# Pricing image parts with TensorE durations from the trace, and Silu and Softplus in halves, in a planned four-layer kernel

## The chip, the cores and the metric

The kernel runs on one core of a Trainium2 chip. The metric is the device time of one execution in microseconds (us). The core has TensorE (PE; its weight loads are shown as PEld), VectorE (DVE), ScalarE (ACT), GpSimd (POOL) and SyncE (SP), each with its own instruction stream that is worked off in order, and DMA queues. Semaphores tie the streams together.

## The reference

The input is a batch of 8 images of 56 x 56 pixels and 192 channels, in float32. Four layers follow each other, each as `x = x + layer(group_norm(x))`:

1. A gated layer with long convolutions: `p = silu(x @ p_w)`, `qv = silu(x @ q_w) * silu(x @ v_w)`, two Toeplitz products of `qv` along the rows and along the columns of the image, `(p * (o1 + o2)) @ o_w`.
2. Attention with 6 heads in shifted windows of 7 x 7 pixels.
3. A depthwise convolution of 3 x 3.
4. A selective scan: a projection to two times 384 channels (`x` and `z`), a depthwise convolution and Silu on `x`, then for each of 4 directions `delta = softplus(dt + bias)`, the recurrence `h = exp(delta * A) * h + (delta * x) * B` along the 3136 tokens for each of 16 states, `y = sum(h * C) + D * x`; the directions are added, normalized, multiplied with `silu(z)` and projected back.

## The kernel before, in words

**Set-up.** The Toeplitz coefficients are made, then `products` and `toeplitz` do the first layer's convolutions for four images; for the other four they run beside the front of the first image.

**The front of an image** is all that has to be done before its scan can start. It is a Python generator, `front(b)`, made of five: `gate` (the rest of layer 1: per chunk of 448 tokens 12 matmuls for `p`, an Identity activation for each of 6 blocks at line 490, one Silu over all six at 492, 48 transposing matmuls at 503, a product on VectorE at 511, 12 matmuls at 516), `attention` (lines 596 to 691), `conv2` (depthwise matmuls at 780), `inner` (input projection at 840, depthwise convolution at 869, two Silu over 3136 tokens at 886, a transposing copy at 892) and `steps` (14 passes: a projection at 918, six small matmuls at 928, six Identity activations at 933, one Softplus over 2688 columns at 937, two stores). After each Silu and Softplus `usual_functions()` (line 342) loads the table that has Exp and Ln again. Each `yield held, needs, wait` ends a part: how many PSUM banks it holds, how many the next part needs, and how long its loads take.

**The scan loop** goes over 8 images x 4 directions ("slots") x 7 chunks = 224 chunks, and in each over 3 blocks of 128 channels and 8 groups of two states: 24 pairs a chunk, 672 an image. For one pair: POOL multiplies `du` with `bm` into one of the 6 slots of `ring` (line 1059), ScalarE sets the initial state (1066, for three pairs at once), forms `exp(delta * A)` in PSUM (1076, two banks' worth of buffers) and keeps the last state (1098); VectorE scans (1085); POOL (for every other pair) or VectorE multiplies the states with `cm` into `hc` (1091, 4 buffers); PE adds them up over the states with an identity matrix (1106, two matmuls that show as four instructions). When a chunk's block is done, `sums` adds it to `ysum` (1116 to 1118). When an image's last direction is under way, `finish` (lines 950 to 1001) normalizes and writes out.

**The planner.** The loop is written out under a manual schedule: what Python emits first stands first in an engine's stream. While it emits pairs, `Parts` keeps a clock for each of the engines P, A, D and E (POOL, ScalarE, VectorE, TensorE) in `self.t`, and `run(engine, cost, *after)` moves one on. The pairs' own costs are written out: 1.78 for POOL, 1.3 for ScalarE's exponentials, 2.02 for a scan, 1.1 for the sum on PE. The costs of the image parts are not: the first image's front runs before the loop, and while it does, every instruction goes through `Meter` and `MeteredEngine`, which note (engine, price) for each part. Those logs are the prices for the fronts of the seven other images. Once a pair, `step` asks `fits` for each open front or finish whether its next part may be emitted now. It may if, with its price added, ScalarE's clock stays 0.7 us before the end of the next scan and TensorE's within 5.0 us after its start; a part that has been refused gets 3 us of grace for each refusal. The next front starts when the one before it has ended. If an image's first `steps` pass is not made when the loop needs it, the front is run on without limits until it is.

The change touches `TIMES`, `call` in `MeteredEngine`, the Silu of `gate` and `inner`, the Softplus of `steps`, the cost in `sums`, and the cost of `add_up` (the `run("E", 1.1, ...)` near the end of the loop).

Of the kernel before, what the change touches and what calls it, by code (L numbers as in the profile page):

```python
# [23 lines left out]
L = H * W  # L24
# [20 lines left out]
class Meter:  # L45


    TIMES = {"tensor": ("E", 0.04, 1.25e-3), "scalar": ("A", 0.2, 0.83e-3),
             "vector": ("D", 0.1, 1.05e-3), "gpsimd": ("P", 0.1, 2.25e-3)}

    def __init__(self, nc):
# [9 lines left out]
class MeteredEngine:  # L61
# [3 lines left out]
    def __getattr__(self, name):  # L65
        f = getattr(self.it, name)
        engine, base, each = self.times

        def call(*args, **kw):
            n, extra = 0, 0.0  # L70
            for v in list(args) + list(kw.values()):
                if hasattr(v, "shape") and (engine != "E" or n == 0):
                    m = 1
                    for s in v.shape[1:]:
                        m *= s
                    n = max(n, m)
            if name == "preload_act_table_set" or AF.Silu in args or AF.Softplus in args:
                extra = 1.28
            if engine == "E" and args[0].shape[0] <= 32:
                n /= 3  # L80
            if name != "dma_start":
                self.meter.log.append((engine, base + each * n + extra))
            return f(*args, **kw)  # L83

        return call
# [3 lines left out]
def model(ctx: ExitStack, tc: tile.TileContext, a: dict, out: bass.AP):  # L89
    nc = tc.nc  # L90
# [213 lines left out]
    with (  # L304
# [144 lines left out]
        def gate(b):  # L449

            w_p, w_o, x, s, ot = carve(slab, TT, (2, D1), (6, C), (2, 2, CH), (6, CH), (2, 2, 4, C))
            w_p, w_o, x, s = w_p[:CP], w_o[:CP], x[:CP], s[:CP]
            nc.sync.dma_start(out=w_p, in_=a["w_p"])
            nc.sync.dma_start(out=w_o, in_=a["w_o"])

            def load_x(j):
                nc.sync.dma_start(out=x[:, j % 2], in_=blocks(a["x"][b])[:, :, j * CH : (j + 1) * CH])

            def load_ot(n):
                j, c = divmod(n, 3)  # L460
                for k in range(2):
                    to, blk = slice(k * CP, (k + 1) * CP), 2 * c + k
                    nc.sync.dma_start(
                        out=ot[:, n % 2, 0, :, to],
                        in_=o_d[0][b][blk, j * CH : (j + 1) * CH, :].rearrange("(t p) c -> p t c", p=TT),
                    )
                    v = o_d[1][b][blk].rearrange("(w h) c -> h w c", h=H)
                    for r in range(2):
                        nc.sync.dma_start(
                            out=ot[r * W : (r + 1) * W, n % 2, 1, :, to],  # L470
                            in_=v[8 * j + r : 8 * j + 8 : 2].rearrange("t w c -> w t c"),
                        )

            load_x(0)
            load_ot(0)
            yield 0, 0, 6.0
            yield from absorb(w_p, stats0[:, b], p_b, nb[:CP, :6], CP, 6)
            for j in range(NCH):
                tok = slice(j * CH, (j + 1) * CH)
                if j + 1 < NCH:  # L480
                    load_x(j + 1)
                for c in range(6):
                    yield 0, 1
                    p = bank()
                    for k in range(2):
                        nc.tensor.matmul(
                            p[:CP, :CH], w_p[:, k, c * CP : (c + 1) * CP], x[:, j % 2, k, :], start=k == 0, stop=k == 1
                        )
                    yield 1, 0
                    nc.scalar.activation(s[:, c, :], p[:CP, :CH], AF.Identity, bias=nb[:CP, c : c + 1])  # L490
                yield 0, 0
                nc.scalar.activation(s, s, AF.Silu)
                usual_functions()
                for c in range(6):
                    n = 3 * j + c // 2
                    if c % 2 == 0 and n + 1 < 3 * NCH:
                        load_ot(n + 1)
                    yield 0, 1

                    p = bank()  # L500
                    for t in range(4):
                        for i in range(2):
                            nc.tensor.matmul(  # L503
                                p[:CP, t * TT : (t + 1) * TT],
                                ot[:, n % 2, i, t, c % 2 * CP : c % 2 * CP + CP],
                                ident[:TT, :TT],
                                start=i == 0,
                                stop=i == 1,
                            )
                    yield 1, 0  # L510
                    nc.vector.tensor_mul(s[:, c, :], s[:, c, :], p[:CP, :CH])  # L511
                for m in range(2):
                    yield 0, 1
                    p = bank()
                    for c in range(6):
                        nc.tensor.matmul(
                            p[:CP, :CH], w_o[:, c, m * CP : (m + 1) * CP], s[:, c, :], start=c == 0, stop=c == 5
                        )
                        if c % 3 == 2:
                            yield 1, 0  # L520
                    xm = x[:, j % 2, m, :]
                    nc.vector.scalar_tensor_tensor(xm, p[:CP, :CH], o_b[:, m : m + 1], xm, ALU.add, ALU.add)
                    nc.vector.bn_stats(out=st[:, m, j, :], in_=xm)
                nc.sync.dma_start(out=blocks(x1_d[b])[:, :, tok], in_=x[:, j % 2])
            yield 0, 0
            yield from group_norm(NCH)
# [272 lines left out]
        def inner(b):  # L799
# [15 lines left out]
            for d in range(ND):  # L815
# [66 lines left out]

                nc.sync.dma_start(out=xT, in_=zr_d[b][:, d, :])
                for src, dst in ((xc, xc_d[0][b]), (xT, z_d[b])):
                    yield 0, 0, 5.0
                    nc.scalar.activation(src, src, AF.Silu)
                    usual_functions()
                    nc.sync.dma_start(out=dst[:, d, :], in_=src)

                for j in range(NCH):  # L890
# [8 lines left out]
        def steps(b):  # L899

            w_x, xc, rc, dl = carve(slab, 128, (2, ND, 128), (2, ND, CH), (2, CH), (2, ND, CH))
            nc.sync.dma_start(out=w_x, in_=a["w_x"])
            todo = [(o, j) for o in (1, 0) for j in range(NCH)]

            def load_x(n):
                o, j = todo[n]
                nc.sync.dma_start(out=xc[:, n % 2], in_=xc_d[o][b][:, :, j * CH : (j + 1) * CH])

            load_x(0)
            yield 0, 0, 8.0  # L910
            for n, (o, j) in enumerate(todo):
                tok = slice(j * CH, (j + 1) * CH)
                if n + 1 < len(todo):
                    load_x(n + 1)
                yield 0, 1
                p = bank()
                for d in range(ND):
                    nc.tensor.matmul(p[:, :CH], w_x[:, o, d, :], xc[:, n % 2, d, :], start=d == 0, stop=d == ND - 1)
                yield 1, 0
                nc.scalar.copy(rc[:, n % 2, :], p[:, :CH])  # L920
                nc.sync.dma_start(out=bc_d[o][b][:, tok], in_=rc[64:, n % 2, :])
                for d in range(ND):
                    yield 0, 2
                    held = []
                    for s in range(2):
                        row = slice(32 * s, 32 * s + R)
                        held.append(bank())
                        nc.tensor.matmul(
                            held[s][:, :CH], w_dt[row, o, d * 128 : (d + 1) * 128], rc[row, n % 2, :], start=True, stop=True
                        )  # L930
                    yield 2, 0
                    for s in range(2):
                        nc.scalar.activation(
                            dl[:, s, d, :], held[s][:, :CH], AF.Identity, bias=dt_b[:, 2 * o + s, d : d + 1]
                        )
                yield 0, 0
                nc.scalar.activation(dl, dl, AF.Softplus)
                usual_functions()
                for s in range(2):
                    nc.sync.dma_start(out=dl_d[2 * o + s][b][:, :, tok], in_=dl[:, s])  # L940
                made.add((b, o, j))
            yield 0, 0
# [167 lines left out]
        def sums(i, d):  # L1110
# [5 lines left out]
                nc.vector.scalar_tensor_tensor(yv, x, Dsum[:, d : d + 1], y, ALU.mult, ALU.add)  # L1116
            else:
                nc.vector.tensor_add(yv, yv, y)
            run("D", 0.87)

        class Parts:

# [101 lines left out]
        with tc.manual_schedule():  # L1224
# [31 lines left out]
            for g, (i, d, k) in enumerate(pairs):  # L1256
# [52 lines left out]
                parts.step({"A": max(n2, fed[g + 2]) - 0.7, "E": n1 + 5.0, "D": 0.2})  # L1309
                if g >= 2:  # L1310
                    add_up(g - 2)
                    summed[g - 2] = run("E", 1.1, taken[g - 2])
            if on_pool(d, k):
                times_c(last)
            for g in (last - 1, last):
# [109 lines left out]
```

## Time and profile before

| what | value |
|---|---|
| median of 7 runs | 21611.34 us (21578.39 to 21635.07) |
| profiled execution | 21578.39 us, span 21576.6 us |
| granted TensorE clock, mean | 0.865 |
| busy | PE 17464.5 (81%), DVE 15782.5 (73%), ACT 12163.8 (56%), POOL 15088.5 (70%) |
| sum over states, line 1106 | 10043.9 us busy, 21504 instructions |
| table loads, line 342 | 189, 1283 ns each |
| table loads before Softplus, line 937 | 98, 1283 ns each |
| Softplus, line 937 | 98 over 2688 columns, 2447 ns each |
| Silu, lines 492 and 886 | 49 over 2688 columns, 2447 ns; 42 over 3136, 2819 ns |

Busy times and shares say how much an engine did, not what it waited for. The profile can be cut into stretches; for each it gives the busy time of every engine, the number of instructions, the granted clock of TensorE and the share of time in which the DMA engines were busy. The list of waits names an instruction and the one that released it: "DVE hc L1091 <- PE ps_y L1106" means that VectorE's product at line 1091 stood still until PE's sum at line 1106 had let go of what it needed. The timeline shows single instructions in order of time.

### The profile page before, as it was taken

To read this page: it belongs to the slowest core of one execution; us is meant where nothing else is said; L and a number is where in the kernel's file an instruction comes from. 1 tells how busy PE (TensorE), PEld (TensorE's weight loads), DVE (VectorE), ACT (ScalarE), POOL (GpSimd) and SP (SyncE) were. 2 spreads that over 40 slices of the span, in tenths; PEclk is the share of its full clock that TensorE was granted. 3 is DMA by queue.
4 is the path that set the end of the run, shared out by engine and by line. 5 is a ranking of instruction groups with operands and counts; after the bars stand their busy time and mean duration, and the time that the engine had idled before them with its cause. 6 is when DMAs were issued, how large, how long until landed. Compare 5 with 4: busy or idle time off the path is not lost. (4 is left out here: it accounts for less than half of the span.)

```text
span 21576.6 us, 198667 instructions
## 1 busy us (share of the span) xinstructions
PE 17464.5 (81%) x59404; PEld 9090.4 (42%) x59404; DVE 15782.5 (73%) x12469; ACT 12163.8 (56%) x28249; POOL 15088.5 (70%) x9176
## 2 busy tenths in 40 slices
PE   7878678887887788878877888788878887777777
PEld 4845455433443344334433444344433443333333
DVE  2122116986798779967896789778977887788998
ACT  3126113666666666656665667476757665755555
POOL 0000005887788778877886789678877887799998
PEclk9587758988998899989998899889988998888888
DMA  3931676456544654475446654665466546544443
GB/s 87 243 98 41 195 210 177 135 159 211 172 137 146 218 174 147 135 221 177 140 137 205 190 142 128 205 198 146 134 202 196 145 133 194 198 135 135 138 136 114
DMA packets 2566491, 3470.12 MB, mean 161 GB/s; under 512 B 936270, under 2 KB 2518704, under 8 KB 2534578
## 3 DMA queue, kind: packets, MB, share of 16 engines
q1 hardware_dynamic: 2542724, 3340.61, 52.0%
q0 software_dynamic: 15520, 116.14, 1.5%
q8 instruction: 473, 7.75, 0.2%
q14 instruction: 606, 4.96, 0.1%
q10 hardware_dynamic: 7168, 0.65, 0.0%
HBM read 2822.68 MB, written 634.11 MB: 160 GB/s over the span
## 5 line engine op out<-in xcount | busy, mean ns | idle before, releaser
L1106 PE MATMUL ps_y<-hc,ident_sb 128*128 128x448 f32 x21504 | 10043.9, 605 | 972.7 <-POOL hc L1091 962.1
L1059 POOL TENSOR_TENSOR ring<-du,bm 128x896 f32<-128x896 f32 x5376 | 9456.5, 1773 | 1852.6 <-ACT ring L1066 1723.5
L1076 ACT ACTIVATE ps_a<-delta,A_logs_sb 128x449 f32<-128x449 f32 x10752 | 6867.0, 639 | 322.5 <-DVE ring L1085 66.3
L1106 PEld LDWEIGHTS ps_y<-hc,ident_sb 128*128 128x128 f32 x21504 | 4327.4, 211 | 5333.9 <-issue 3586.4
L1085 DVE TENSOR_TENSOR_SCAN ps_a<-ps_a,ring 128x898 f32<-128x898 f32 x2688 | 5430.3, 2020 | 929.3 <-ACT ring L1066 485.7
L1085 DVE TENSOR_TENSOR_SCAN ring<-ps_a,ring 128x898 f32<-128x898 f32 x2688 | 5423.3, 2018 | 498.5 <-ACT state L1098 197.6
L1091 POOL TENSOR_TENSOR hc<-ring,cm 128x896 f32<-128x896 f32 x2688 | 4762.7, 1772 | 877.2 <-DVE ring L1085 488.1
L1091 DVE TENSOR_TENSOR hc<-ps_a,cm 128x896 f32<-128x896 f32 x2688 | 2935.1, 1092 | 933.5 <-PE ps_y L1106 704.3
L1098 ACT COPY state<-ps_a 128x2 f32<-128x2 f32 x2687 | 427.2, 159 | 2967.2 <-DVE hc L1091 2960.4
L287 DVE COPY tzx<-ps_tz 112x448 f32<-112x448 f32 x432 | 269.9, 625 | 1442.7 <-PE ps_tz L281 1287.8
L281 PE MATMUL ps_tz<-tzx,tm 112*112 112x112 f32 x4608 | 1031.0, 406 | 339.9 <-DMA tm<-ext 291.5
L295 POOL DMA_DIRECT2D o<-tzx x192 | 97.4, 514 | 1580.7 <-DVE tzx L287 1448.3
L281 PEld LDWEIGHTS ps_tz<-tzx,tm 112*112 112x112 f32 x4608 | 1021.7, 319 | 380.4 <-issue 376.7
L1098 ACT COPY state<-ring 128x2 f32<-128x2 f32 x2688 | 506.3, 188 | 657.0 <-DVE ring L1085 636.2
L666 PE MATMUL ps_f<-ident_sb,slab 98*98 98x98 f32 x1344 | 332.9, 328 | 637.2 <-ACT slab L659 634.8
L1042 POOL TENSOR_TENSOR du<-delta,xcd 128x448 f32<-128x448 f32 x672 | 658.3, 980 | 21.7 <-DMA slab<-o 21.3
L83 PE MATMUL ps_f<-slab 96*32 96x448 f32 (+7 forms) x2432 | 596.1, 563 | 69.2 <-DMA slab<-pad 49.3
L1066 ACT COPY ring<-state 128x6 f32<-128x6 f32 x1536 | 294.3, 192 | 631.1 <-POOL ring L1059 629.6
L666 PEld LDWEIGHTS ps_f<-ident_sb,slab 98*98 98x98 f32 x1344 | 204.7, 159 | 1040.6 <-ACT slab L659 818.9
L234 PE MATMUL ps_qv<-wqv,xn 96*128 96x384 f32 (+1 forms) x1200 | 527.1, 522 | 132.9 <-DVE xn L153 67.7
L503 PEld LDWEIGHTS ps_f<-ident_sb,slab 112*96 112x96 f32 x4704 | 509.4, 169 | 238.4 <-issue 108.6
L503 PE MATMUL ps_f<-ident_sb,slab 112*96 112x112 f32 x4704 | 530.6, 267 | 97.0 <-DVE slab L511 53.9
(221 smaller groups left out, 16265.8 us busy)
## 6 DMA issues: line engine op xcount, KB each, us to landing
bm<-bc SPq DMA_DIRECT2D x1792, 448.0 KB
cm<-bc SPq DMA_DIRECT2D x1792, 448.0 KB
xcd<-xc SPq DMA_DIRECT2D x840, 224.0 KB
dl<-slab SPq DMA_DIRECT2D x224, 672.0 KB
delta<-dl SPq DMA_DIRECT2D x224, 672.0 KB
slab<-pad SPq DMA_DIRECT2D x504, 232.0 KB
tzx<-qv SPq DMA_DIRECT2D x192, 588.0 KB
o<-tzx POOLq DMA_DIRECT2D x192, 588.0 KB, 14.1
```

The source lines that it names most:

```text
L83: return f(*args, **kw)
L234: nc.tensor.matmul(pq[:p_t], xn[:CP, 0, tok], wqv[:CP, 0, col], start=True, stop=False)
L281: nc.tensor.matmul(po[:, c, :], t[:, :, c2 + c], x[:, :, c1 + c2 + c], start=True, stop=True)
L503: nc.tensor.matmul(p[:CP, t * TT : (t + 1) * TT], ot[:, n % 2, i, t, c % 2 * CP : c % 2 * CP + CP], ident[:TT, :TT], start=i == 0, stop=i ...
L666: nc.tensor.transpose(p[:PT_, e * PT_ : (e + 1) * PT_], S[:, 3 * g + e, :], ident[:PT_, :PT_])
L1042: nc.gpsimd.tensor_mul(du[:, 0, :], deltas[i][:, d, 1 : CH + 1], xcs.pop((i, d)))
L1059: nc.gpsimd.tensor_mul(hs[:, :, tokens(i)[0]], dus[i, d].to_broadcast([128, NG, CH]), bms[i, k])
L1076: nc.scalar.activation(dA[:, n, :], deltas[i][:, d, at : at + CH + 1], AF.Exp, scale=negA[:, slot, d, c : c + 1])
L1085: nc.vector.tensor_tensor_scan(h, dA, hs, 0.0, ALU.mult, ALU.add)
L1091: (nc.gpsimd if on_pool(d, k) else nc.vector).tensor_mul(hc, h[:, :, tokens(i)[0]], cms[i, k])
L1098: nc.scalar.copy(states[i][:, d, NG * k : NG * k + NG], h[:, :, tokens(i)[2]])
L1106: nc.tensor.matmul(yps[i, d][:, :CH], ident, hcs[g][:, n, :], start=k + n == 0, stop=k + n == NP + NG - 2)
```

## The change

TensorE's parts get prices of their own. An instruction with `n` output columns cost `0.04 + 1.25e-3 * n` (with `n` a third for an output of up to 32 partitions); it now costs the larger of 0.16 and `1.68e-3 * n`, a third of that for an output of up to 32 partitions, and half for a contraction over up to 32 rows and for a transpose. A pair's sum on PE costs 1.5 instead of 1.1. The row sums on VectorE cost 1.0 for the slots 2 and 3 and 0.7 for 0 and 1, instead of 0.87.

Each Silu of the front becomes two, over half of the columns each, and each Softplus two, one for each direction. The usual table is loaded after each half, and each half is a part of its own for the planner. In `steps` the store of a direction follows its half.

```diff
-    TIMES = {"tensor": ("E", 0.04, 1.25e-3), "scalar": ("A", 0.2, 0.83e-3),
+    TIMES = {"tensor": ("E", 0.0, 0.0), "scalar": ("A", 0.2, 0.83e-3),
              "vector": ("D", 0.1, 1.05e-3), "gpsimd": ("P", 0.1, 2.25e-3)}
...
-            if engine == "E" and args[0].shape[0] <= 32:
-                n /= 3
+            if engine == "E":
+                m, k = args[0].shape[0], args[1].shape[0]
+                us = max(0.16, 1.68e-3 * n) / (3 if m <= 32 else 2 if k <= 32 or name == "transpose" else 1)
+                self.meter.log.append((engine, us))
+                return f(*args, **kw)
...
-                yield 0, 0
-                nc.scalar.activation(s, s, AF.Silu)
-                usual_functions()
+                for c in (0, 3):
+                    yield 0, 0
+                    nc.scalar.activation(s[:, c : c + 3], s[:, c : c + 3], AF.Silu)
+                    usual_functions()
...
-                    yield 0, 0, 5.0
-                    nc.scalar.activation(src, src, AF.Silu)
-                    usual_functions()
+                    for u in range(2):
+                        yield 0, 0, 0.0 if u else 5.0
+                        half = src[:, u * (L // 2) : (u + 1) * (L // 2)]
+                        nc.scalar.activation(half, half, AF.Silu)
+                        usual_functions()
...
-                yield 0, 0
-                nc.scalar.activation(dl, dl, AF.Softplus)
-                usual_functions()
                 for s in range(2):
+                    yield 0, 0
+                    nc.scalar.activation(dl[:, s], dl[:, s], AF.Softplus)
+                    usual_functions()
                     nc.sync.dma_start(out=dl_d[2 * o + s][b][:, :, tok], in_=dl[:, s])
...
-            run("D", 0.87)
+            run("D", 1.0 if slot >= 2 else 0.7)
...
-                    summed[g - 2] = run("E", 1.1, taken[g - 2])
+                    summed[g - 2] = run("E", 1.5, taken[g - 2])
```

## The prediction

> **What bounds the kernel now.** I read the slices of the page first: up to 3420 us the parts of the first image are done and the first layer of all images is begun and ended; then the scan loop runs to 21541 us. One pass of that loop is a "pair" (two states of one block of 128 channels, one chunk of 448 tokens); there are 8 x 672 = 5376, so a pair takes 18121 / 5376 = 3.37 us. I then cut the loop into stages, with the lines of the image parts as marks: 9960 to 12165 us holds one whole front (the parts of one image, woven between the pairs of the image before), in the order gate, attention, conv2, inner, steps. The last row, 20000 to 20810, has pairs alone.
>
> ```profile
> core 0: us, PE busy (x) PEld busy (x) DVE busy (x) ACT busy (x) POOL busy (x), PEclk, DMA share, GB/s
> 9960.00:10470.00 510.00, 473.09 (x1810) 274.51 (x1810) 407.30 (x312) 286.32 (x588) 398.75 (x244) 0.97 0.51 143
> 10470.00:11285.00 815.00, 669.16 (x2381) 333.65 (x2379) 758.15 (x632) 565.60 (x1650) 722.12 (x432) 0.90 0.43 133
> 11285.00:11445.00 160.00, 108.06 (x388) 38.55 (x389) 119.47 (x108) 60.20 (x137) 97.89 (x58) 0.84 0.74 203
> 11445.00:11865.00 420.00, 322.29 (x1141) 141.32 (x1139) 290.90 (x191) 243.72 (x483) 300.01 (x179) 0.87 0.68 211
> 11865.00:12165.00 300.00, 257.12 (x596) 105.50 (x596) 219.41 (x140) 241.57 (x423) 232.19 (x139) 0.84 0.61 211
> 20000.00:20810.00 810.00, 582.87 (x1171) 251.07 (x1171) 761.48 (x479) 427.77 (x979) 798.27 (x480) 0.87 0.41 132
> ```
>
> With pairs alone POOL is busy 798 of 810 us: it is the bound there. In the front it is busy 72 to 89%, so something stops it: PE is at 93% in gate, ACT at 81% in steps, DMA at 68 to 74% in conv2 and inner. The same stretches, for the scans alone (one per pair):
>
> ```profile
> 9960.00:10470.00 510.00, 274.55 (x137) 0.97 0.51 143
> 10470.00:11285.00 815.00, 527.28 (x264) 0.90 0.43 133
> 11285.00:11445.00 160.00, 70.24 (x35) 0.84 0.74 203
> 11445.00:11865.00 420.00, 222.70 (x111) 0.87 0.68 211
> 11865.00:12165.00 300.00, 169.93 (x86) 0.84 0.61 211
> 20000.00:20810.00 810.00, 585.91 (x295) 0.87 0.41 132
> ```
>
> Pairs alone take 810 / 295 = 2.746 us. Against that rate the stages lose 510 - 137 x 2.746 = 134 us (gate), 90 (attention), 64 (conv2), 115 (inner), 64 (steps): 467 us a front, some 3270 us for the seven that lie in the loop. That is all this change can play for. A front takes 633 pairs and has 672, so it runs ahead of its due time by some 39 pairs an image. Third view, the waits in the same front:
>
> ```profile
> POOL ring L1059 <- ACT ring L1066: 245.0, 120, 15.2
> ...
> DVE hc L1091 <- PE ps_y L1106: 104.2, 75, 10.8
> POOL hc L1091 <- DVE ring L1085: 85.1, 33, 13.1
> ...
> ACT slab L879 <- PE ps_f L869: 54.3, 16, 8.3
> ...
> ACT slab L490 <- PE ps_f L486: 46.7, 33, 5.1
> ```
>
> POOL mostly waits for ACT, and ACT, which works in order, stands at copies of image parts whose matmuls are not done; VectorE waits for PE to free its products (`hc`, four buffers). So PE runs later than the order of the instructions assumed.
>
> **Part 1, the prices of TensorE.** Prices add no instruction; they change where the planner puts image parts. It used 1.1 us for a pair's four-instruction sum. The trace has 232.50 us for 547 such instructions in gate (another answer of the same stretch, line 1106), 1.70 us a pair at a granted clock of 0.97, and 582.87 / 293 = 1.99 at 0.87. The new 1.5 is nearer and still low. From the code, the price of a front's PE work goes, old to new, from 162 to 192 (gate: per chunk 24 matmuls of 448 columns, 0.60 to 0.753, and 48 of 112, 0.18 to 0.188), 147 to 129 (attention), 29 to 32, 108 to 128, 76 to 63 (steps): 522 to 544 in all. So in gate the planner held PE to be busy for 162 + 137 x 1.1 = 313 of 510 us, and will now count 397, where the trace has 473 (with the finish parts, which come beside). Its limit of 5 us of work ahead of the scan will bind, and gate spreads over more pairs: I estimate 20 (15%). In gate PE is the bound: its time is (473 - 137 x 1.70 = 240) + 1.70 for each pair, over 0.93, so another pair costs 1.83 us there and saves 2.746 later: 20 x 0.92 = 18 us a front. In inner and conv2 the pace falls by some tenth; I take a quarter of the 104 us for which VectorE waited for PE, 27 us a front, since the waits of PE for DMA (25.1 us at line 869, 29.6 at line 780) are behind much of it and no price knows of them. Sum: 45 us a front, **315 us** for seven. Bounds: 0 (ACT's limit, not PE's, sets the order), and all 104 us, 730.
>
> **Part 2, halves.** Per image 7 Silu in gate, 6 in inner and 14 Softplus in steps become two each, with the table of Exp and Ln loaded between: 27 more switches, 189 in the loop. One block today, ScalarE's rows:
>
> ```profile
> 9722.93 1.28 ACT L937 ACT_TABLE_LOAD   x1
> 9724.23 2.45 ACT L937 ACTIVATE slab<-slab 128x2688 f32<-128x2688 f32 x1
> 9726.69 1.28 ACT L342 ACT_TABLE_LOAD   x1
> ```
>
> It holds ScalarE for 5.04 us. The groups give 2447 ns for 2688 columns and 2819 for 3136: 0.83 ns a column and 216 ns fixed. A half of 2688 columns takes 1.33 us and its block 3.93. So ScalarE works 189 x (2.57 + 0.22) = 527 us longer in the loop. What a block costs the loop is read from POOL's gaps around five Softplus blocks (9702 to 9797 us): 0.74 + 2.20 + 0.36; 0.53 + 2.18 + 0.38; 1.45 + 0.38; 0.60 + 0.36; 2.33 + 2.19 + 0.35: 2.8 us in the mean. So 5.04 - 2.8 = 2.2 us are covered by work done ahead. If each half has the same cover it costs 3.93 - 2.2 = 1.7 us, two 3.4 to 3.5: about 0.7 more a split, 189 x 0.7 = **132 us lost**, my value: the nearest rows are those gaps. Bounds: if the planner finds room so that a half costs 1 us, 2 - 2.8 = -0.8 a split, a gain of 151; if a half costs as much as a whole, 2.8 x 189 = 529 lost. In steps ScalarE is at 81% and its price per step goes from 9.2 to 12.1 us, so steps takes some 20 pairs more; with gate's 20 and about 10 of inner that makes 633 + 50 = 683 pairs for 672. The first of the 14 steps is what an image waits for, some 100 pairs before the front's end, so seven fronts of 11 pairs too many (77) are still in time.
>
> The stores go with the halves: in steps the first of the two `dl` stores is issued one half sooner and the second one half later; both wait on SyncE's queue, in order, for ScalarE, and behind them stand the loads of `bm` and `cm` (line 1027) for a chunk 24 pairs ahead. That distance, some 70 us, hides 4 us; the one row of this kind, POOL waiting for `bm`, stood for 6.0 us in 700 (9000 to 9700), so without cover it is at most some 20 us a front. The Silu stores still follow both halves.
>
> In the first front, which no pair accompanies, the Softplus rows near 3029 and 3050 us have no table load beside them, and ScalarE is idle for most of that time (45.85 of 300 us busy from 2900 on): 0 to 40 us, I take 10. The prices of a row sum (0.87 to 1.0 or 0.7) even out (0.13 up for half of the slots, 0.17 down for the rest, three sums a chunk): nothing, and if that cover fails, 0.17 x 3 x 224 = 114 us at most either way.
>
> The Trainium skill speaks against this half of the change: "ScalarE: Activation LUTs", section Table sets: the hidden batching unit, says to do all calls of one table set together, and What ACT_TABLE_LOAD costs gives 1283 ns for a load and 1380 more for a drain at each switch. The trace agrees on the load (1283 ns) but shows 0.02 us between it and its neighbours, no drain; by the page's figure the added ScalarE work would be 189 x (2 x 2.66 + 0.22) = 1047 us and not 527, an estimate that these rows contradict.
>
> **Sum.** -315 + 132 + 10 = -173 us. The profiled execution took 21578.39 us (span 21576.6, 1.8 around it), so it would take 21405; the median of the seven runs is 33 above it, so the forecast is 21611 - 173 = 21440 us.
>
> **Rivals.**
> - *Each half stalls like a whole* (slower). Place: behind every Silu and Softplus, POOL at line 1059 waiting for ScalarE's line 1066. For it: the planner grants a shorter block a slot sooner, with less work done ahead; ScalarE is at 81% in steps. Against: the block is 1.1 us shorter. 529 + 10 - 315 = +224: 21835 us. It decides from the point where a split costs over (315 - 10) / 189 = 1.6 us, a half over 2.2.
> - *The fronts come too late* (about the same, or slower). If a front takes 710 pairs, not 683, 38 x 7 = 266 are missing at the end, some 110 of them covered by the hundred pairs named above; the rest of the front is then run with no pair beside it. Its PE work (767 us in `ps_f` over the front) and ScalarE's (1397 - 633 x 1.5 = 447) come to 1.9 us a pair in one chain: 156 x 1.9 = 300. -173 + 300 = +127: 21740.
> - *PE's lateness was most of it*: all 104 us a front go: -730 + 142 = -588: 21020.
> - *The prices do nothing*, since ACT's limit sets the order: only the halves are left, +142: 21750.
>
> **How the numbers follow.** The forecast gets 0.45 (alone it spans 21300 to 21600: 0.38 faster, 0.07 within 0.2%), stalling halves 0.20 (slower), late fronts 0.12 (0.02 faster, 0.04 same, 0.06 slower), the large gain 0.15 (faster), no effect 0.08 (slower). Faster 0.55, same 0.11, slower 0.34; 0.2% (43 us) is about what a measurement of this kernel can tell from no change. The range goes from 21000, at the large gain, to 21850, past the stalling halves.
>
> **What would show it.** Right: loads at line 342 go from 189 to some 378; gate takes about 157 pairs and a front some 680, so pairs alone remain only in the last image; "DVE hc <- PE ps_y" falls by a third or more; POOL's gap around a half is under 2.2 us. Wrong: POOL waiting longer for line 1066 in steps; a stretch of image parts without scans at an image's end; gate's pair count unchanged.

## The result, and the profile after

| | median | ratio to before, 95% interval |
|---|---|---|
| before | 21617.53 us (61 runs) | |
| changed kernel | 21657.8 us (25 runs) | 1.0016 (1.0011 to 1.0022) |

The forecast was 21440 us, 0.8% faster; the change makes the kernel 40 us slower, within the 0.2% that the prediction calls no change. That is no absence of effects: the profile below shows, in one front, a gain and a loss of some hundred microseconds each that cancel.

The page of the changed kernel, in the order busy time, busy share, group rows (busy us, mean ns | idle time before them, and who ended it). Its line numbers are 3 to 6 higher than before: 1065 is the old 1059, 1072 the old 1066, 1097 the old 1091, 345 the old 342.

```profile
span 21668.1 us, 199535 instructions
...
PE 17391.7 (80%) x59404; PEld 9112.7 (42%) x59404; DVE 15795.4 (73%) x12469; ACT 12714.8 (59%) x28862; POOL 15088.0 (70%) x9176
...
L1065 POOL TENSOR_TENSOR ring<-du,bm 128x896 f32<-128x896 f32 x5376 | 9457.9, 1773 | 2261.7 <-ACT ring L1072 2043.1
...
L1097 POOL TENSOR_TENSOR hc<-ring,cm 128x896 f32<-128x896 f32 x2688 | 4762.3, 1772 | 556.3 <-PE ps_y L1112 195.8
```

The same two lines of POOL before, and VectorE's product, which is needed further down:

```profile
L1059 POOL TENSOR_TENSOR ring<-du,bm 128x896 f32<-128x896 f32 x5376 | 9456.5, 1773 | 1852.6 <-ACT ring L1066 1723.5
L1091 POOL TENSOR_TENSOR hc<-ring,cm 128x896 f32<-128x896 f32 x2688 | 4762.7, 1772 | 877.2 <-DVE ring L1085 488.1
L1091 DVE TENSOR_TENSOR hc<-ps_a,cm 128x896 f32<-128x896 f32 x2688 | 2935.1, 1092 | 933.5 <-PE ps_y L1106 704.3
```

ScalarE works 551 us longer (12163.8 before). POOL, the bound, stands 409 us longer ahead of its first product (1852.6 to 2261.7), 320 of them behind ScalarE (1723.5 to 2043.1), and 321 us less ahead of its second (877.2 to 556.3): one queue got worse, the other better. The table loads have doubled as announced:

```profile
L345 ACT ACT_TABLE_LOAD x378 | 485.0, 1283 | 6.3
```

To see where, I cut the loop at each part's first instruction on ScalarE or VectorE and count scans. Front 4 before, then the same front of the changed kernel (gate, attention, conv2, inner, steps; stretch, its length, scan time and number of scans, clock, DMA):

```profile
9965.00:10497.00 532.00, 282.22 (x141) 0.95 0.52 146
10497.00:11282.00 785.00, 514.84 (x258) 0.91 0.42 130
11282.00:11455.00 173.00, 77.44 (x39) 0.85 0.71 196
11455.00:11875.00 420.00, 219.74 (x110) 0.86 0.70 217
11875.00:12180.00 305.00, 172.15 (x87) 0.83 0.63 212
```

```profile
10615.00:11094.00 479.00, 297.75 (x149) 0.95 0.55 158
11094.00:11866.00 772.00, 515.71 (x258) 0.92 0.42 130
11866.00:12047.00 181.00, 96.68 (x49) 0.86 0.71 202
12047.00:12561.00 514.00, 238.92 (x119) 0.85 0.66 199
12561.00:12953.00 392.00, 199.43 (x99) 0.81 0.58 185
```

Against 2.746 us for a pair alone the losses were 532 - 141 x 2.746 = 145, 77, 66, 118 and 66 us, 472 in all; now they are 70, 64, 46, 187 and 120, 487 in all. In this front gate, attention and conv2 gain 108 us, inner and steps lose 123. Front 4 is not the mean: over all seven fronts, cut in the same way with each scan counted where it starts, the first three gain 533 us and the other two lose 621. At the end of inner and into steps lies a stretch with no scan at all. POOL's timeline there, after its last multiplication:

```profile
12507.65 1.77 POOL L1065 TENSOR_TENSOR ring<-du,bm 128x896 f32<-128x896 f32 x1
12577.99 1.77 POOL L1065 TENSOR_TENSOR ring<-du,bm 128x896 f32<-128x896 f32 x1 [68.57 <-ACT ring L1072]
```

Such a gap of 68.6 to 69.0 us stands in front of the last pairs of the images 3 to 6 of 0 to 7, at 12578, 14915, 17257 and 19595 us; before there is none above 20 us. ScalarE in that gap runs the last third of the front's inner and the first pass of steps, with a table load on each side of each half though nothing stands between them (five of its rows):

```profile
12519.28 1.28 ACT L892 ACT_TABLE_LOAD   x1
12520.58 1.51 ACT L892 ACTIVATE slab<-slab 128x1568 f32<-128x1568 f32 x1
12522.11 1.28 ACT L345 ACT_TABLE_LOAD   x1
12523.40 1.28 ACT L892 ACT_TABLE_LOAD   x1
12524.69 1.51 ACT L892 ACTIVATE slab<-slab 128x1568 f32<-128x1568 f32 x1
```

That is the loop running a late front to its due point with no pair beside it. The loads are a small part of the gap: from 12505 to 12580 us ScalarE is busy for 41.5 of 75 us, and the rest of the time it waits, for matmuls and transfers of that front. Besides, the loop's first scan comes at 3495 us, 76 us later than before.

**Theory L.** The prices gain, the halves cost some, and both together make a front too long for its image, so it comes late. **Rival S.** Each half stalls like a whole, and the prices are worth little. **W1 and W2**: the later start comes from the prices, by which the share of other images' work beside the first front is reckoned, or from the halves in the first front itself.

### The profile page after: what moved, and what is told of

Same layout as the page of the kernel before. It is cut to its first block, busy times and chain, and to the rows that moved or that the text cites. A ratio compares the mean times of both kernels' runs of the same rounds, so it can differ in the third digit from the quotient of the medians.

```text
span 21668.1 us, 199535 instructions
## 1 busy us (share of the span) xinstructions
PE 17391.7 (80%) x59404; PEld 9112.7 (42%) x59404; DVE 15795.4 (73%) x12469; ACT 12714.8 (59%) x28862; POOL 15088.0 (70%) x9176
## 5 line engine op out<-in xcount | busy, mean ns | idle before, releaser
L1065 POOL TENSOR_TENSOR ring<-du,bm 128x896 f32<-128x896 f32 x5376 | 9457.9, 1773 | 2261.7 <-ACT ring L1072 2043.1
L1112 PE MATMUL ps_y<-hc,ident_sb 128*128 128x448 f32 x21504 | 9897.8, 599 | 649.3 <-POOL hc L1097 640.1
L1097 POOL TENSOR_TENSOR hc<-ring,cm 128x896 f32<-128x896 f32 x2688 | 4762.3, 1772 | 556.3 <-PE ps_y L1112 195.8
L934 PE MATMUL ps_f<-slab,w_dt_sb 12*128 12x448 f32 x1176 | 411.7, 752 | 355.0 <-ACT slab L926 335.7
```

What stands on the lines that cost most here:

```text
L1065: nc.gpsimd.tensor_mul(hs[:, :, tokens(i)[0]], dus[i, d].to_broadcast([128, NG, CH]), bms[i, k])
L1097: (nc.gpsimd if on_pool(d, k) else nc.vector).tensor_mul(hc, h[:, :, tokens(i)[0]], cms[i, k])
L1112: nc.tensor.matmul(yps[i, d][:, :CH], ident, hcs[g][:, n, :], start=k + n == 0, stop=k + n == NP + NG - 2)
```

## Experiments

Each difference in us below is to the median of the kernel before in the same session (21623 for the first four, 21610 for the next four, 21661 for the last three).

**1. The new prices alone** (the changed kernel with whole Silu and Softplus).

```diff
-                for c in (0, 3):
-                    yield 0, 0
-                    nc.scalar.activation(s[:, c : c + 3], s[:, c : c + 3], AF.Silu)
-                    usual_functions()
+                yield 0, 0
+                nc.scalar.activation(s, s, AF.Silu)
+                usual_functions()
...
```

> The new prices alone; Silu and Softplus whole as before. Theory L (late fronts: the changed kernel's fronts of 698 pairs do not fit in 672, and the halves are what make them too long): fronts of about 670 pairs, no stretch of more than 20 us without a scan, gate, attention and conv2 as cheap as in the changed kernel (together 533 us less than before over seven fronts), inner and steps no dearer than before; about 21617 - 533 + 76 (the later start of the loop, if that comes from the prices) = 21160 us, ratio 0.979. Theory S (each half stalls like a whole, the prices are worth little, at most the 315 us of the prediction): 21300 to 21550. No effect of the prices: 21617.

Measured: 21244.22 us, ratio 0.9821 (0.9806 to 0.9835), 379 us faster. Front 4 of this kernel, the same five stages:

```profile
10258.00:10744.00 486.00, 293.56 (x148) 0.96 0.60 166
10744.00:11524.00 780.00, 516.68 (x258) 0.91 0.40 124
11524.00:11707.00 183.00, 95.07 (x48) 0.84 0.68 192
11707.00:12161.00 454.00, 245.83 (x123) 0.87 0.72 222
12161.00:12514.00 353.00, 187.94 (x94) 0.88 0.62 202
```

671 pairs; losses 80, 72, 51, 116 and 95, 414 in all. So gate, attention and conv2 gain 85 us here from the prices alone; inner costs what it did, steps 29 more. POOL has no gap over 20 us. But the row that the prediction named, VectorE's, has hardly moved:

```profile
L1094 POOL TENSOR_TENSOR hc<-ring,cm 128x896 f32<-128x896 f32 x2688 | 4762.9, 1772 | 622.3 <-DVE ring L1088 219.0
L1094 DVE TENSOR_TENSOR hc<-ps_a,cm 128x896 f32<-128x896 f32 x2688 | 2935.2, 1092 | 951.5 <-PE ps_y L1109 719.2
```

VectorE waits 719.2 us for PE over the run, against 704.3 before (in front 4 alone 87.4 against 104.1). What fell is POOL's idle time ahead of its product (877.2 to 622.3), above all its wait for the scan (488.1 to 219.0). Theory L had expected 21160 us, a somewhat larger gain; S allowed 315 us at most.

**2. The halves alone** (the kernel before with the three halved activations).

```diff
-                yield 0, 0
-                nc.scalar.activation(dl, dl, AF.Softplus)
-                usual_functions()
                 for s in range(2):
+                    yield 0, 0
+                    nc.scalar.activation(dl[:, s], dl[:, s], AF.Softplus)
+                    usual_functions()
...
```

> The halves alone, with the old prices. Theory L: fronts of some 657 pairs, below 672, so none is late; only the cost of a split is left, 0.7 us x 189 = 132 us as the prediction has it: 21750, ratio 1.006. Theory S: 189 x 2.8 = 529 us: 22150, ratio 1.024. If the halves help by themselves: below 21570.

Measured: 21905.94 us, ratio 1.0131 (1.0118 to 1.0145), 283 us slower: 1.5 us a split, between L's 0.7 and S's 2.8. No gap, no late front. ScalarE's rows for the Softplus halves:

```profile
L941 ACT ACTIVATE slab<-slab 128x1344 f32<-128x1344 f32 x196 | 259.8, 1326 | 2.2
L941 ACT ACT_TABLE_LOAD x196 | 251.5, 1283 | 3.4
```

A half takes 1.33 us as reckoned; with two loads it holds ScalarE for 3.92 us. Neither size of a split was right. And 1.5 us is a mean over all 189, not what happens at each: cut into stages like front 4, the seven gates lose 778 us against 769 before, inner 917 against 864, steps 903 against 534, and attention, which has no half, 558 against 658. By these sums a Softplus split costs 3.8 us, by front 1 alone, which starts alike in both kernels, 1.3 (steps lose 136 against 118): what a stage loses also depends on where in the image it falls. The sum of runs 1 and 2, -379 + 283 = -96, is not the changed kernel's +40: 136 us come only when both are there.

**3. The first front's share by the old prices**, the rest as in the changed kernel.

```diff
+                self.meter.old += 0.04 + 1.25e-3 * (n / 3 if m <= 32 else n)
...
-                spent += 0.55 * sum(cost for _, cost in log[-1])
+                spent += 0.55 * meter.old
+                meter.old = 0.0
```

> The changed kernel, except that the share of other images' convolutions that is put beside the first front is still reckoned with the old TensorE prices (the loop's own prices stay new). Theory W1 (the loop starts 76 us later, at 3495 instead of 3420 us, because the new prices move that share): the loop starts near 3420 again, 21658 - 75 = 21583 us. Theory W2 (the halves lengthen the first front itself, whose parts then follow one another): the start stays near 3495 and the time near 21658.

Measured: 21630.64 us, ratio 1.0005 (0.9996 to 1.0013): 7 us over before, where the changed kernel is 40 over. The loop starts at about 3450 us: 45 of the 76 us are gone, and 30 stay. W1 and W2 both have a part. Neither part is fixed: the start is at 3426 us with the prices alone and 3439 with the halves alone.

**4. Softplus whole**, Silu in halves, all new prices (the steps edit of run 2, undone in the changed kernel).

> The changed kernel with Softplus whole again; Silu stays in halves. Theory L: fronts of about 683 pairs, no front late by the end of the run since an image waits for the first of 14 passes only, so no stretch of 65 us without scans; steps as cheap as before (536 us of excess over seven fronts instead of 836): 21658 - 300 - 4 x 65 + some tens for a shorter run of pairs alone = 21100 to 21250. Theory S: 98 of the 189 splits are gone, 98 x 2.8 = 274 less: 21380.

Measured: 21349.83 us, ratio 0.9874 (0.986 to 0.9887), 273 us faster than before and some 310 faster than the changed kernel. POOL has no gap over 20 us; fronts are 669 to 684 pairs long. L's range was 21100 to 21250, S's value 21380: the number sits nearer S, the missing gaps and the unlate fronts are L's. The 91 Silu splits cost 106 us over run 1, 18 of them by a later start of the loop: 1.0 us a split in the mean.

**5 and 6. Which price.** Run 5 is the kernel before with

```diff
-                    summed[g - 2] = run("E", 1.1, taken[g - 2])
+                    summed[g - 2] = run("E", 1.5, taken[g - 2])
```

and run 6 is run 1 with this line at 1.1 again.

> The kernel before with one edit: a pair's sum on TensorE is priced 1.5 instead of 1.1; image parts keep their old prices, Silu and Softplus stay whole. If the gain of the prices (379 us) comes from counting the pairs' own matmuls: 21250 to 21350. If it comes from the image parts' prices: near 21600. Fronts of some 648 pairs, none late.

Measured: 21517.85 us, ratio 0.9956 (0.9939 to 0.9972), 93 us faster.

> The image parts' new TensorE prices and the new row-sum prices, but a pair's sum still at 1.1; Silu and Softplus whole. The complement of the run with the pair's price alone: if the image prices carry the gain, 21250 to 21350; if the pair's price does, near 21600. The two together made 21244. Fronts of some 660 pairs, none late.

Measured: 21354.57 us, ratio 0.9878 (0.9862 to 0.9893), 256 us faster. The two nearly add up to run 1 (349 of 379): the image parts' prices, with those of the row sums, which this run changes too, carry two thirds. In the prediction the sum of a front's prices hardly moved (522 to 544); what moved is which part is dear, and gate, conv2 and inner are then spread over more pairs.

**7. Late fronts without halves**: run 1 with TensorE's limit at 2.5 us.

```diff
-                parts.step({"A": max(n2, fed[g + 2]) - 0.7, "E": n1 + 5.0, "D": 0.2})
+                parts.step({"A": max(n2, fed[g + 2]) - 0.7, "E": n1 + 2.5, "D": 0.2})
```

> All new prices, Silu and Softplus whole (21244 us with 670 pairs a front), and TensorE's limit at 2.5 us instead of 5.0, so that a front wants about 705 pairs and comes late without any half. Theory L (lateness costs by itself, in a stretch without scans at an image's end): stretches of some 40 to 65 us without a scan from the second or third image on and 40 to 60 us a front more than the run with 5.0, for four to six fronts: 21450 to 21550. If lateness costs nothing, and only the halves do: 21200 to 21300 with the stretches there.

Measured: 21352.9 us, ratio 0.9877 (0.9861 to 0.9894), 258 us faster than before: 121 us less gain than run 1. POOL stands still for 62 to 67 us at the end of five images (10110, 12409, 14701, 16997, 19295 us), so lateness needs no half. One of these:

```profile
12408.71 1.77 POOL L1062 TENSOR_TENSOR ring<-du,bm 128x896 f32<-128x896 f32 x1 [62.15 <-ACT ring L1069]
```

The time is below L's 21450 to 21550. The likely reason is that the lower limit by itself gains: run 10, with 3.5 us, is faster than run 1, and in this run gate and conv2 lose 164 us less over the seven fronts than in run 1, while inner loses 332 more.

**8. Only gate's Silu in halves**, new prices (the inner and steps edits undone).

> All new prices, Silu of gate in halves, Silu of inner and Softplus whole: 49 of the 189 splits, fronts of some 673 pairs, none late. By 0.7 us a split: 21244 + 34 = 21280. By 1.5 us a split, what the halves alone cost: 21244 + 74 = 21320. By 2.8: 21380. Gate is held up by TensorE, so it may be less than any of these.

Measured: 21329.39 us, ratio 0.9861 (0.9836 to 0.9885): 98 us less gain than run 1. The loop starts at 3472 us, 45 later than in run 1; the remaining 53 are 1.1 us for each of the 49 splits, again as a mean. They do not fall where the halves are: the seven gates lose 523 us against 527 in run 1, but inner 916 against 863 and steps 712 against 688.

**9. The changed kernel with a lead**: the second front's gate runs ahead of the first pair.

```diff
-            ahead_of, b_next = None, 1
             ending, anything = None, dict.fromkeys("ADE", 1e9)
+            ahead_of, b_next = parts.add(front(1), "front"), 2
+            while ahead_of.at < 233:
+                parts.step(anything, ahead_of)
```

> The changed kernel, all halves and all prices, but the gate of the second image's front is run with no pair beside it ahead of the loop's first pair, so that the fronts are some 150 pairs ahead and never late. In the changed kernel the fronts 4 to 7, which are late, lose 491 to 497 us each against pairs alone, the fronts 1 to 3 434 to 466. Theory L: no stretch of over 20 us without a scan after the first pairs, fronts 4 to 7 lose 430 to 470 us each, some 40 less; the lead costs its own 200 to 300 us once and saves the first gate's 64, so 21658 + 190 - 4 x 45 = 21670 us, give or take 60. If the later fronts are dear for another reason (each half stalls like a whole): the stretches vanish, the fronts still lose about 490 us, and the time is 21850.

Measured: 21642.82 us, ratio 0.9995 (0.9985 to 1.0004). POOL's only gap over 20 us is the lead's:

```profile
3700.06 1.77 POOL L1097 TENSOR_TENSOR hc<-ring,cm 128x896 f32<-128x896 f32 x1 [211.04 <-DVE ring L1091]
```

and front 4 of this kernel reads

```profile
10297.00:10833.00 536.00, 322.00 (x161) 0.97 0.54 155
10833.00:11617.00 784.00, 515.66 (x258) 0.91 0.42 129
11617.00:11801.00 184.00, 95.12 (x48) 0.83 0.67 191
11801.00:12257.00 456.00, 253.94 (x127) 0.86 0.71 215
12257.00:12687.00 430.00, 223.75 (x111) 0.87 0.59 186
```

705 pairs; losses 94, 76, 52, 107 and 125: 454, where the changed kernel had 487. With the gap gone inner is back at 107. The lead stood 211 us, of which some 64 had been lost in the first gate anyway, and still the kernel is no slower than the changed one: four late fronts cost about what the lead costs. The time is within 60 us of L's 21670. S expected 490 us a front and 21850; it falls for the late fronts. Gate costs 24 us more here (94 against 70), so the saving in inner is not all kept. Steps stays dear, 125 against 95 in run 1: halves without lateness.

**10. A version that beats both**: run 1 with TensorE's limit at 3.5 us in the line of run 7.

> All new prices, Silu and Softplus whole, TensorE's limit 3.5 us instead of 5.0: fronts of some 680 pairs, still not late at the end. If TensorE standing too far ahead is what is left of the loss in gate and steps, and fronts are not late: 21130 to 21200, better than 21244. If fronts begin to be late: 21250 to 21350.

Measured: 21180.86 us, ratio 0.9784 (0.9771 to 0.9797), the fastest here. No gap over 20 us.

**11. The pair's sum at 1.7 us** in run 1.

> All new prices, Silu and Softplus whole, and a pair's sum at 1.7 us, which the trace of before has in gate, instead of 1.5: fronts of some 672 pairs. The step from 1.1 to 1.5 was worth 110 us; if the gain goes on: 21180 to 21230. If it is used up: 21244 to 21280.

Measured: 21330.23 us, ratio 0.9851 (0.9837 to 0.9864), 330 us faster than before, against run 1's 379, and above both expected ranges. The two intervals only just part, so all this shows is that a price nearer to the trace's 1.70 us brought nothing more. The length of a front is not the reason: 669 to 672 pairs here, 667 to 672 in run 1. The cause is open.

## Why the prediction was wrong, step by step

- **Bound, stages and what can be won**: right. Fronts, not pairs, hold the loss, and POOL waits for ScalarE in them. Two slips change nothing: POOL is busy for 61% of conv2 and 71% of inner, not 72 to 89% everywhere, and a quarter of 104 us is 26, not 27.
- **Part 1, prices: the total right, the reason not.** 315 us forecast, 379 measured (run 1). The step "a quarter of the 104 us for which VectorE waited for PE" failed: over the run that wait stayed (704.3 to 719.2 us). What came instead is more gain in gate than its 18 us a front (seven gates: 769 to 527 us, 35 a front), and gains in attention and conv2 that I had not counted (198 us over seven fronts); steps lose 154 more. That the total came near is luck in part. Run 6 shows the image parts' prices, with the row sums', as the larger share. Why the new order gains is not shown beyond this. The mean granted clock of TensorE moves too (0.865 before, 0.870 in run 1, 0.860 in the changed kernel); whether that is a cause or follows from the order was not tried.
- **Part 2, halves: mis-sized.** The term was 0.7 us a split, 132 us; measured are, as means, 1.5 with the old prices (run 2) and 1.0 to 1.1 with the new, for Silu (runs 4 and 8). The block's length was right (3.93 against 3.92 us). The failed step is "if each half has the same cover": a cover of 2.2 us for each half would leave 1.7; two halves cost 2.8 + 1.5 = 4.3 together, 2.1 each. Read in the prediction's own terms a half so finds less work done ahead, 1.8 us of it; but this is a reading and not shown, since run 8 loses its time in stages that have no half, and in run 2 the price differs from stage to stage. The rival of whole stalls (2.8 a split) fell as a mean of all splits; for the Softplus halves with the old prices the stage sums of run 2 leave it open.
- **The front's length: too short, and enough to turn the sign.** "633 + 50 = 683 pairs", "still in time". The first two fronts took 698: gate and steps 13 and 23 pairs more, about the 20 each that I gave them, but inner 23 and not 10, and conv2 9 and not 0. That is 26 pairs too many a front where the prediction had 11; three fronts use up 80 of the hundred pairs that it counted as spare, and from the fourth on each comes late. My own rival of late fronts had this mechanism, at 710 pairs and 300 us of standing still; it happened in four fronts of seven, with 275 us of gaps, and the sign named for it, a stretch without scans at an image's end, is in the profile. Its net price is not measured by itself. One estimate is the part of the 136 us of run 2's sum that the later start doesn't explain: the start is 76 us later with both changes, against 7 and 20 with each alone, so 49; some 87 remain. The other is run 9: 33 us less for front 4, four times which is 132.
- **The first front: mis-sized.** I took 10 us; the loop starts 76 us later. Run 3 gives 45 of them to the share of other images' work that is put beside it, which moves with the prices. I had looked only at the added loads there.
- **The row sums' prices** were changed together with the image parts' prices in run 6 and not tried alone: what they did is open.
- **The drain**: the Trainium skill ("ScalarE: Activation LUTs", What ACT_TABLE_LOAD costs) has 2.66 us for a switch, with a drain. No run shows the drain; the 378 loads of line 345 have 6.3 us of idle time before them in all. The rule of the same page (Table sets: the hidden batching unit) to keep one table set together agrees with both pairs of runs here: run 1 is faster than the changed kernel, and the kernel before faster than run 2.

Sum over run 1: the changed kernel is 379 + 40 = 419 us behind it. 69 are the later start (3495 - 3426), 87 to 132 the late fronts by the two estimates, and 218 to 263 are left for 189 splits, 1.2 to 1.4 each, which fits the means of runs 2, 4 and 8. Against the forecast of -173 us, the prices gave 64 more, and the splits cost 86 to 131 more, the start 59 more and the late fronts 87 to 132 that were not in the sum. Each of the last three is larger than the 40 us by which the sign is wrong.

## What to carry to other kernels

When work is woven into a loop by prices, two limits act at once: how much a part disturbs the loop, and how many passes it takes. Before an edit that makes parts dearer or more numerous, reckon the passes for every stage and hold them against the due time; here there was a lead of 39 pairs of 672 an image, and some hundred once at the end. And try the edits of one change apart: 1.8% gain and 1.3% loss stood in one diff.

## What the runs showed of the hardware that was not expected

A table load that follows another at once, with nothing between that uses the first, still takes its full time: 1.28 us at 12522.11 and again at 12523.40. In that late front four half Silu so hold ScalarE with eight loads, 10.3 us, where two whole ones would have four.
